# A fused two-layer graph network: another order of the second layer's matmul steps, and other places for its side work

## The chip, the cores and the metric

The kernel runs on one core of a Trainium2 chip. The metric is device time in microseconds; the time before is the median of three runs. A profile is one more execution, recorded instruction by instruction.

The engines are called as the profile calls them: PE is TensorE's matmul, PEld its weight load (the two overlap), DVE is VectorE, ACT ScalarE, POOL GpSimd, and SP the queue that issues nearly all transfers. Each engine works through its own list in order. They meet through semaphores. Matmuls write to PSUM, which has eight banks of 128 x 512 fp32; only DVE and ACT read PSUM back into SBUF.

## The reference

128 graphs of 128 nodes with 512 features, all fp32. Layer 0 is a mean over neighbours, layer 1 a diffusion with attention-like weights; each is followed by a residual and a layer norm.

```python
# layer 0: x = layernorm(x + gnn0(x, adj, W))
deg = jnp.sum(adj, axis=-1, keepdims=True)
agg = jnp.einsum('bij,bjf->bif', adj, x) / jnp.maximum(deg, EPS)
cat = jnp.concatenate([x, agg], axis=2)
out = jax.nn.relu(jnp.einsum('bnf,of->bno', cat, W))

# layer 1: x = layernorm(x + gnn1(x, adj, ...))
Xw = X @ Wv + bv
sj, si = Xw @ aw[:d, 0], Xw @ aw[d:, 0]
e = leaky_relu(sj[:, None, :] + si[:, :, None] + ab[0], 0.2)
alpha = A * jnp.exp(e)
transition = alpha / (jnp.sum(alpha, axis=-1, keepdims=True) + 1e-12)
H, Xk = 0, X
for k in range(3):
    H = H + Xk @ Wk[k] + bk[k]
    Xk = jnp.einsum('bij,bjd->bid', transition, Xk)
out = jax.nn.relu(H)
```

## The kernel before

Four graphs make a group; there are 32 groups (`NG`). Layer 0 goes through all of them, then layer 1. The result of layer 0 goes to memory (`yds`) and comes back.

**Products.** The wide product of layer 1 (x with the three matrices `Wk` and two score columns, laid out as 4 x 385 columns) is computed with seven block products in place of eight, each of which again has seven inner products in place of eight. The outer products are the generators `o1` to `o7`, all made by `outer`. An inner product is one *step*: one matmul of 128 x 128 by 128 x 385, which the profile records as two weight loads and two matmuls. `O5.3` is the third step of outer product 5.

A product works in the four banks of its *lane*, called X, Y, W, Z: lane 1 (the banks `bA`) runs O1, O5, O7 and the combine, lane 0 (`bB`) runs O2, O6, O4 and O3. In `outer` the seven steps do this:

1. X gets the first inner product; ACT copies it to Y (L628). In O5 ACT has first put the bias into X (L626).
2. Z gets one; it goes to SBUF as `s5` (ACT L634, or DVE L632 in O5).
3. X accumulates; DVE writes X + s5 to W (L637).
4. Y accumulates and is evicted (ACT L660, or DVE L669).
5. X accumulates and is read by `direct` (DVE L663 or L676).
6. W accumulates and is evicted.
7. X accumulates and is evicted.

So X is written in steps 1, 3, 5 and 7, and each of the reads between has to end before the next write. Then the banks change roles: the next product on the lane begins in this one's Y.

`combine` (steps c.1 to c.8, 512 columns wide) applies the transition matrix twice to each of four graphs: first result plus `r` or `c` into `v1` (DVE L846, L847), a copy of the base into PSUM (ACT L849), second result on top, and then the residual with ReLU and row sums (DVE L380).

**Order.** Nothing is scheduled automatically: the program walks through a list of steps written by hand and calls the generators, so PE's order is the list's. `PG` serves group 0 of layer 1, `PB` groups 1 to 30, and `PL` the last one. In `PB` the lower-case names (`c.`, and `o3.7`) belong to the group before. Each list of `PB` has 57 steps: 49 products and 8 of the combine; I call it a round.

**Side work.** Everything else has a *place*: twice the number of the step, counted from the round's first step, after which it is issued; an even place comes before the evictions that a step leaves to `late`, an odd one after. A round is 114 places, so place 243 of one round is place 15 of the round after the next. `PLACES_B` holds them. The names:

- `load_left`, `load_y`, `load_adj`: transfers in, on SP (tiles `xb`, `y`, `ag`); `y_store`: the transfer out.
- `x_turn` (DVE L259) turns blocks of x; `x_inner`, `x_s1` to `x_s4` (POOL) make the sums of x that the block products need.
- `sum_r`, `sum_c` (POOL) add the block products `s` onto `r` and `c22`.
- `t_scores` (ACT L725, L726, DVE L734, one store), `t_load` (the load of `T`, L792), `t_exp` (ACT L799, L800), `t_sums` (POOL L805, DVE L807, L810, ACT L808), `t_norm` (ACT L817 and a store to `sd`), `t_back` (loads of `sb`), `t_turn` (DVE L825): they make the transition matrix `TT` for the next round's combine.
- `ln_mean`, `ln_scales` (POOL L499, L510 to L512), `ln_var` (ACT L504), `ln_apply` (ACT L517): the layer norm of rows that the combine has finished.

Of the kernel before, what the change touches and what calls it, by code (L numbers as in the profile page):

```python
# [16 lines left out]
def kernel(  # L17
# [853 lines left out]
    def step(lane, name, g, k):  # L871
        steps.append((lane, name, g, k))
# [4 lines left out]
    PG = ("O5.1 O5.2 O2.5 O5.3 O5.4 O6.1 O2.6 O5.5 O6.2 O5.6 O5.7 O6.3 O7.1 O7.2 O6.4 "  # L877
          "O6.5 O2.7 O7.3 O6.6 O6.7 O7.4 O4.1 O7.5 O4.2 O4.3 O7.6 O4.4 O4.5 O7.7 O4.6 "
          "c.1 c.2 c.3 O4.7 O3.1 c.4 O3.2 c.5 c.6 c.7 O3.3 O3.4 c.8 O3.5 O3.6").split()
    PB = ("O1.1 O1.2 o3.7 O1.3 O2.1 O1.4 O1.5 O2.2 O1.6 O1.7 O2.3 O2.4 O5.1 O2.5 O2.6 O5.2 O5.3 O5.4 O2.7 "  # L880
          "O6.1 O5.5 O6.2 O6.3 O5.6 O5.7 O6.4 O7.1 O7.2 O6.5 O6.6 O7.3 O6.7 O7.4 O4.1 O7.5 O4.2 O4.3 O7.6 "
          "O4.4 O4.5 O7.7 O4.6 c.1 O4.7 O3.1 c.2 O3.2 O3.3 c.3 c.4 c.5 c.6 c.7 c.8 O3.4 O3.5 O3.6").split()
    PL = ("O1.1 o3.7 O1.2 O1.3 O2.1 O2.2 O1.4 O1.5 O1.6 O1.7 O2.3 O2.4 O5.1 O2.5 O2.6 O5.2 O5.3 O5.4 O2.7 O6.1 O5.5 O6.2 "
          "O5.6 O5.7 O6.3 O7.1 O6.4 O6.5 O7.2 O7.3 O6.6 O7.4 O7.5 O6.7 O7.6 O7.7 O3.1 O3.2 O3.3 O3.4 c.1 c.2 c.3 c.4 "
          "c.5 c.6 c.7 c.8 O4.1 O3.5 O4.2 O3.6 O3.7 O4.3 O4.4 O4.5 O4.6 O4.7 x.1 x.2 x.3 x.4 x.5 x.6 x.7 x.8").split()
# [15 lines left out]
    for s in PT:  # L901
        name, k = s.split(".")
        step(int(not s[0].isupper()), {"p74": "P74", "t": "T"}.get(name, name), 0 if s[0] == "O" else NG - 1, int(k))
    base[NG] = len(steps) - PB.index("O5.1")
    LANE = {"O1": 1, "O2": 0, "O5": 1, "O6": 0, "O7": 1, "O4": 0, "C": 1, "O3": 0}
    for g in range(NG):
        base[NG + g] = base[NG] + len(PB) * g
        for s in PL if g == NG - 1 else PB if g else PG:
            name, k = s.split(".")
# [18 lines left out]
    def place_op(n, pos, name, m, *a):  # L928
# [28 lines left out]
        ("a_load", 0): 81, ("load_adj", 1): 43, ("y_store", 0, 0): 161, ("load_y", 0, 0): 105, ("ln_apply", 0, 0): 145,  # L957
    }
    PLACES_B = {
        ("x_s1", 1): 63, ("t_back", 0): 168, ("x_turn", 1, 1, 1): 21, ("ln_apply", 0, 0): 243, ("ln_var", 0, 1): 226,  # L960
        ("x_s2", 1): 79, ("t_scores", 0): 120, ("t_norm", 0): 154, ("sum_r", 0, 0): 85, ("y_store", 0, 0): 275,
        ("t_turn", 0): 189, ("ln_var", 0, 2): 224, ("sum_c", 0, 0): 114, ("x_turn", 1, 0, 0): 11, ("ln_apply", 0, 3): 263,
        ("ln_var", 0, 0): 232, ("t_exp", 0): 143, ("load_left", 2, 1): 68, ("load_y", 0, 0): 175, ("ln_apply", 0, 1): 258,
        ("x_s3", 1): 79, ("sum_r", 0, 1): 87, ("x_inner", 1, 0): 46, ("x_s4", 0): 53, ("x_turn", 1, 0, 1): 27,
        ("t_load", 0): 129, ("ln_apply", 0, 2): 274, ("load_adj", 0): 106, ("load_left", 2, 0): 75, ("load_y", 0, 1): 185,
        ("x_inner", 1, 1): 52, ("ln_scales", 0): 240, ("y_store", 0, 1): 286, ("t_sums", 0): 153, ("x_turn", 1, 1, 0): -4,
        ("ln_mean", 0): 223, ("ln_var", 0, 3): 228, ("sum_c", 0, 1): 110,
    }
    PLACES_M = {
        ("y_store", 0): 250, ("ln_mean",): 214, ("ln_apply", 0): 241, ("ln_apply", 3): 242, ("ln_var", 3): 225,  # L970
# [130 lines left out]
```

## Time and profile before

| | |
|---|---|
| median of three runs | 2068.39 us (2068.28 to 2069.03) |
| the profiled execution, its own time | 2068.23 us |
| its span, first to last instruction | 2066.5 us |
| mean granted TensorE clock | 0.999 |
| layer 1, 830 to 2000 us: PE busy | 1169.93 of 1170.00 us |
| the same stretch: PEld, DVE, ACT, POOL busy | 649.35, 824.49, 612.68, 728.82 us |
| the same stretch: DMA share, moved | 0.47, 109 GB/s |

A row of the timeline gives the start and the length in us, the engine, the line, the operation with its output and inputs, and how many equal instructions in a row were merged (x4). In brackets stands the time that the engine was idle before the row, with what ended it; "issue" is idle time for which the profile shows no releaser. Idle times below 0.15 us are not listed, and the ends of matmuls are modelled, so PE shows as busy across short gaps.

### The profile page before, as it was taken

What the parts mean: (1) busy time and instruction counts of PE and PEld (TensorE: products, weight loads), DVE (VectorE), ACT (ScalarE), POOL (GpSimd) and SP (SyncE); (2) the same over time, 40 slices, a digit from 0 to 9 for tenths busy, and PEclk for the clock granted to TensorE, in tenths of its full rate; (3) what the DMA queues carried; (4) which work ended last, traced back from release to release, by engine and by line L of the source; (5) the groups of instructions that cost most, each with busy time, mean ns of one, the idle gap of its engine ahead of it and who ended that gap; (6) DMA issues with size and microseconds to landing.
All of it is one profiled execution on the core that took longest, in us unless ns stands there. A gap on an engine that the chain in (4) does not pass through costs nothing.

```text
span 2066.5 us, 25981 instructions
## 1 busy us (share of the span) xinstructions
PE 2053.8 (99%) x7108; PEld 1338.4 (65%) x7108; DVE 1515.5 (73%) x3418; ACT 1161.4 (56%) x2872; POOL 1374.6 (67%) x1263
## 2 busy tenths in 40 slices
PE   9999999999999999999999999999999999999998
PEld 6878888888887887555555555555555555555554
DVE  6787777787878777667767767767766766766766
ACT  2666666666666666455455455455455455455454
POOL 5877888887777776756656656656656656656652
PEclk9999999999999999999999999999999999999999
DMA  9777766666667777434534534534534534534623
GB/s 202 176 192 189 187 188 176 158 190 190 165 162 197 181 189 228 108 88 112 129 88 109 132 88 112 128 88 112 128 88 113 128 88 113 128 87 112 129 75 110
DMA packets 431071, 287.14 MB, mean 139 GB/s; under 512 B 155593, under 2 KB 353865, under 8 KB 430924
## 3 DMA queue, kind: packets, MB, share of 16 engines
q1 hardware_dynamic: 429996, 284.15, 55.6%
q10 hardware_dynamic: 800, 1.31, 0.3%
q8 instruction: 56, 0.92, 0.2%
q14 instruction: 91, 0.75, 0.1%
q0 software_dynamic: 128, 0.01, 0.0%
HBM read 191.60 MB, written 93.79 MB: 138 GB/s over the span
## 4 chain that ended last, share of the span: by engine, by line
PE 98%; DMA 1%; DVE 1%; issue 0%; POOL 0%; ACT 0%; ACTq 0%; SPq 0%; DVEq 0%
PE bA L155 51%; PE bB L155 47%; DMA xb<-in_x_dram 0%; DMA big<-in_w0t_dram 0%; PE bA L181 0%; DVE big L1024 0%; DVE c L458 0%; PE bA L167 0%; DVE c L366 0%; ACT y L562 0%; POOL rs L539 0%; DVE dg L730 0%; DVE bA L475 0%; DVE y L380 0%; DVE xl L259 0%
## 5 line engine op out<-in xcount | busy, mean ns | idle before, releaser
L155 PE MATMUL bB<-big,xu 128*128 128x385 f32 (+1 forms) x1806 | 556.8, 433 | 0.1
L155 PEld LDWEIGHTS bB<-big,xu 128*128 128x128 f32 x1806 | 342.6, 190 | 159.8 <-issue 24.4
L155 PE MATMUL bA<-big,xl 128*128 128x256 f32 (+1 forms) x1358 | 406.0, 416 | 0.6 <-DVE bA L475 0.6
L155 PE MATMUL bB<-big,xs 128*128 128x256 f32 (+1 forms) x1316 | 389.0, 416 | 0.0
L155 PEld LDWEIGHTS bA<-big,xl 128*128 128x128 f32 x1358 | 256.5, 189 | 100.5 <-issue 15.3
L155 PEld LDWEIGHTS bB<-big,xs 128*128 128x128 f32 x1316 | 249.6, 190 | 84.1 <-issue 1.7
L155 PE MATMUL bA<-big,xu 128*128 128x256 f32 (+1 forms) x896 | 287.0, 432 | 0.1
L155 PE MATMUL bA<-c,TT 128*128 128x512 f32 x512 | 240.7, 592 | 0.0
L504 ACT ACTIVATE junk<-y,mv 128x512 bf16<-128x512 f32 x252 | 181.7, 721 | 88.9 <-POOL mv L499 82.6
L499 POOL TENSOR_SCALAR mv<-mv 128x4 f32<-128x4 f32 x63 | 14.4, 228 | 313.0 <-DVE y L380 313.0
L155 PEld LDWEIGHTS bA<-big,xu 128*128 128x128 f32 x896 | 166.5, 189 | 76.6 <-DVE bA L397 5.0
L517 ACT ACTIVATE y<-y,mv,rstd 128x512 f32<-128x512 f32 x252 | 204.7, 814 | 3.6 <-POOL mv L512 1.7
L637 DVE TENSOR_TENSOR bB<-bB,s 128x385 f32<-128x385 f32 x128 | 72.6, 567 | 170.9 <-ACT s L634 73.4
L380 DVE SCALAR_TENSOR_TENSOR y<-bA,y 128x512 f32<-128x512 f32 x253 | 165.7, 681 | 12.0 <-PE bA L155 7.4
L155 PE MATMUL bB<-big,xl 128*128 128x385 f32 (+1 forms) x462 | 172.1, 480 | 0.4 <-ACT bA L456 0.4
L805 POOL TENSOR_TENSOR T<-ag,T 128x512 f32<-128x512 f32 x31 | 39.5, 1274 | 198.7 <-ACT T L800 145.8
L155 PE MATMUL bA<-big,xs 128*128 128x385 f32 x448 | 167.9, 491 | 0.0
L155 PEld LDWEIGHTS bA<-c,TT 128*128 128x128 f32 x512 | 96.8, 189 | 88.8 <-issue 47.6
L270 POOL TENSOR_TENSOR xs<-xl 128x896 f32<-128x896 f32 x63 | 131.4, 2085 | 21.4 <-PE bB L155 21.4
L849 ACT COPY bA<-r 128x512 f32<-128x512 f32 x62 | 36.5, 589 | 190.7 <-DVE big L847 190.6
L282 POOL TENSOR_TENSOR xu<-xu,xs 128x896 f32<-128x896 f32 x63 | 131.5, 2087 | 9.3 <-PE bB L155 9.3
L278 POOL TENSOR_TENSOR xl<-xu,xl 128x896 f32<-128x896 f32 x63 | 133.4, 2117 | 1.1
(206 smaller groups left out, 3614.2 us busy)
## 6 DMA issues: line engine op xcount, KB each, us to landing
xb<-in_x_dram SPq DMA_DIRECT2D x256, 128.0 KB, 3.8
y<-in_x_dram SPq DMA_DIRECT2D x64, 512.0 KB, 4.3
yd<-y SPq DMA_DIRECT2D x64, 512.0 KB, 3.0
xb<-yd SPq DMA_DIRECT2D x256, 128.0 KB, 6.5
y<-yd SPq DMA_DIRECT2D x64, 512.0 KB, 6.8
out_dram<-y SPq DMA_DIRECT2D x62, 512.0 KB, 3.3
ag<-in_adj_dram SPq DMA_DIRECT2D x63, 256.0 KB, 6.0
sb<-sd SPq DMA_DIRECT2D x252, 64.0 KB, 3.3
```

Of the source, the lines that this page charges most:

```text
L155: nc.tensor.matmul(dst, lhsT, rhs, start=start, stop=True, skip_group_check=True)
L270: S_.tensor_add(xs[n][:, 0], xl[n][:, 0], xl[n][:, 1])
L278: S_.tensor_sub(xl[n][:, 0], xu[n][:, 0], xl[n][:, 0])
L282: S_.tensor_sub(xu[n][:, 1], xu[n][:, 1], xs[n][:, 1])
L380: V.scalar_tensor_tensor(y, t, 0.0, y, ALU.max, ALU.add, accum_out=mvs[n][:, b, 0:1])
L499: S_.tensor_scalar(mvs[n][:, :, 0], mvs[n][:, :, 0], -1.0 / F, None, ALU.mult)
L504: L_.activation(junk, ys[n, b // 2][:, b % 2], AF.Square, bias=mvs[n][:, b, 0:1], accum_out=mvs[n][:, b, 1:2])
L517: L_.activation(y, y, AF.Identity, bias=mvs[n][:, b, 0:1], scale=rstds[n][:, b : b + 1])
L637: V.tensor_add(W, X, s5)
L805: S_.tensor_mul(T, adjs[NG + g], T)
L849: L_.copy(to[b], row(b, 254, 766, 1))
```

## The change

The list `PB` is replaced by another order of the same 57 steps, and `PLACES_B` by other places for the same pieces of side work. `PG`, `PL`, the other tables of places and all the functions stay as they are. The entries of `PLACES_B` are written in another order, which means nothing.

```diff
-    PB = ("O1.1 O1.2 o3.7 O1.3 O2.1 O1.4 O1.5 O2.2 O1.6 O1.7 O2.3 O2.4 O5.1 O2.5 O2.6 O5.2 O5.3 O5.4 O2.7 "
-          "O6.1 O5.5 O6.2 O6.3 O5.6 O5.7 O6.4 O7.1 O7.2 O6.5 O6.6 O7.3 O6.7 O7.4 O4.1 O7.5 O4.2 O4.3 O7.6 "
-          "O4.4 O4.5 O7.7 O4.6 c.1 O4.7 O3.1 c.2 O3.2 O3.3 c.3 c.4 c.5 c.6 c.7 c.8 O3.4 O3.5 O3.6").split()
+    PB = ("O1.1 o3.7 O1.2 O1.3 O1.4 O2.1 O2.2 O1.5 O1.6 O1.7 O2.3 O2.4 O5.1 O2.5 O5.2 O5.3 O2.6 O2.7 O6.1 "
+          "O5.4 O5.5 O6.2 O5.6 O6.3 O5.7 O6.4 O7.1 O6.5 O6.6 O7.2 O7.3 O6.7 O4.1 O7.4 O7.5 O4.2 O4.3 O7.6 "
+          "O4.4 O4.5 O7.7 O4.6 c.1 O4.7 O3.1 c.2 O3.2 c.3 O3.3 c.4 c.5 c.6 c.7 c.8 O3.4 O3.5 O3.6").split()
```

```diff
     PLACES_B = {
-        ("x_s1", 1): 63, ("t_back", 0): 168, ("x_turn", 1, 1, 1): 21, ("ln_apply", 0, 0): 243, ("ln_var", 0, 1): 226,
-        ("x_s2", 1): 79, ("t_scores", 0): 120, ("t_norm", 0): 154, ("sum_r", 0, 0): 85, ("y_store", 0, 0): 275,
-        ("t_turn", 0): 189, ("ln_var", 0, 2): 224, ("sum_c", 0, 0): 114, ("x_turn", 1, 0, 0): 11, ("ln_apply", 0, 3): 263,
-        ("ln_var", 0, 0): 232, ("t_exp", 0): 143, ("load_left", 2, 1): 68, ("load_y", 0, 0): 175, ("ln_apply", 0, 1): 258,
-        ("x_s3", 1): 79, ("sum_r", 0, 1): 87, ("x_inner", 1, 0): 46, ("x_s4", 0): 53, ("x_turn", 1, 0, 1): 27,
-        ("t_load", 0): 129, ("ln_apply", 0, 2): 274, ("load_adj", 0): 106, ("load_left", 2, 0): 75, ("load_y", 0, 1): 185,
-        ("x_inner", 1, 1): 52, ("ln_scales", 0): 240, ("y_store", 0, 1): 286, ("t_sums", 0): 153, ("x_turn", 1, 1, 0): -4,
-        ("ln_mean", 0): 223, ("ln_var", 0, 3): 228, ("sum_c", 0, 1): 110,
+        ("ln_apply", 0, 1): 257, ("ln_var", 0, 3): 227, ("t_scores", 0): 121, ("x_turn", 1, 0, 1): 26, ("x_s1", 1): 65,
+        ("t_back", 0): 164, ("x_turn", 1, 1, 1): 25, ("x_inner", 1, 1): 63, ("sum_r", 0, 1): 86, ("t_turn", 0): 189,
+        ("ln_var", 0, 1): 225, ("x_s2", 1): 80, ("t_norm", 0): 155, ("y_store", 0, 1): 287, ("sum_r", 0, 0): 84,
+        ("sum_c", 0, 0): 116, ("x_turn", 1, 0, 0): 10, ("ln_apply", 0, 3): 257, ("ln_var", 0, 0): 233, ("t_exp", 0): 138,
+        ("load_left", 2, 1): 86, ("y_store", 0, 0): 261, ("t_load", 0): 128, ("load_y", 0, 0): 179, ("x_s3", 1): 74,
+        ("x_inner", 1, 0): 52, ("ln_apply", 0, 2): 284, ("ln_var", 0, 2): 228, ("load_adj", 0): 116, ("x_s4", 0): 50,
+        ("load_left", 2, 0): 57, ("load_y", 0, 1): 187, ("ln_mean", 0): 221, ("ln_scales", 0): 241, ("t_sums", 0): 151,
+        ("ln_apply", 0, 0): 244, ("x_turn", 1, 1, 0): 6, ("sum_c", 0, 1): 97,
     }
```

## The prediction

> **What bounds the kernel now.** I read the page first, then the list of waits, then the chain in order of time, and then two short stretches of the timeline: an ordinary round of the second layer and its last round.
>
> ```profile
> span 2066.5 us, 25981 instructions
> ...
> PE 2053.8 (99%) x7108; PEld 1338.4 (65%) x7108; DVE 1515.5 (73%) x3418; ACT 1161.4 (56%) x2872; POOL 1374.6 (67%) x1263
> ...
> PE 98%; DMA 1%; DVE 1%; issue 0%; POOL 0%; ACT 0%; ACTq 0%; SPq 0%; DVEq 0%
> ```
>
> TensorE is the bound, and by the page it is never idle. The chain in order of time gives the length of a round: the twelve matmul records at the end of a combine (c.3 to c.8) begin once a round.
>
> ```profile
> 1339.41 5.15 PE bA L155 x12
> ...
> 1378.13 5.15 PE bA L155 x12
> ```
>
> That is 38.72 us a round. What would it be with no loss at all? Four records take 1.29 us (any "x4" row of the chain), so one step of 385 columns, two records, takes 0.647 us; six steps of 512 columns take 5.15, so one takes 0.858. A round has 49 of the first and 8 of the second: 31.70 + 6.86 = 38.57. So a round loses about 0.16 us that no busy share shows, and this is all there is to win. An ordinary round shows where:
>
> ```profile
> 1504.52 1.46 PE L155 MATMUL bA<-big,xu 128*128 128x385 f32 x4
> ...
> 1506.01 0.56 DVE L663 TENSOR_TENSOR r<-bA,s 128x385 f32<-128x385 f32 x1 [0.27 <-PE bA L155]
> ...
> 1507.03 0.81 ACT L517 ACTIVATE y<-y,mv,rstd 128x512 f32<-128x512 f32 x1
> ...
> 1507.75 0.85 ACT L660 COPY r<-bA 128x385 f32<-128x385 f32 x2
> 1507.75 1.46 PE L155 MATMUL bB<-big,xu 128*128 128x385 f32 x4
> ...
> 1508.48 0.50 ACT L626 COPY bA<-beta 128x385 f32<-128x385 f32 x1
> ...
> 1509.10 0.30 PEld L155 LDWEIGHTS bA<-big,xs 128*128 128x128 f32 x2 [0.51 <-issue]
> ```
>
> L626 puts the bias into the bank of O5.1. ScalarE reaches it late, behind the normalisation L517 and two evictions L660, and ends at 1508.98. O5.1 was due at 1507.75 + 4 x 0.3235 = 1509.04; its weights load at 1509.10, and the matmul after it comes at 1509.85 where 1507.75 + 6 x 0.3235 = 1509.69 was due: 0.16 lost. (It is the same in every round: among the weight loads from 890 to 1960 us, the group bA<-big,xs idles 13.7 us before its loads without a named releaser, 27 times this 0.51.) So this copy has to end 0.22 us before the slot to cost nothing. The same stretch shows O1.5 (from 1505.17) read by L663 until 1506.57, and O1.7, which writes the same bank again, not due before 1507.11: no loss.
>
> The last round runs another list (PL), in which only O1.6 stands between O1.5 and O1.7:
>
> ```profile
> 2008.76 3.02 PE L155 MATMUL bA<-big,xu 128*128 128x385 f32 x8
> ...
> 2010.25 0.56 DVE L663 TENSOR_TENSOR r<-bA,s 128x385 f32<-128x385 f32 x1 [1.44 <-PE bA L155]
> ...
> 2010.86 0.30 PEld L155 LDWEIGHTS bA<-big,xu 128*128 128x128 f32 x2 [0.62 <-DVE r L663]
> ...
> 2011.62 1.46 PE L155 MATMUL bB<-big,xu 128*128 128x385 f32 x4
> 2011.82 0.48 ACT L660 COPY r<-bA 128x385 f32<-128x385 f32 x1 [0.44 <-PE bA L155]
> 2012.19 0.49 ACT L626 COPY bA<-beta 128x385 f32<-128x385 f32 x1
> ```
>
> The four steps O1.4 to O1.7 begin at 2008.76 and O2.3 was due at 2008.76 + 4 x 0.647 = 2011.35; it begins at 2011.62. The wait for L663 cost 0.27 us.
>
> **The change, part by part.** No instruction is added or removed. PB serves 30 rounds (groups 1 to 30), so 0.14 us a round is 4.1 us, which is 0.2%.
>
> *O1.5 to O1.7.* Old list: O1.5 O2.2 O1.6 O1.7. New list: O1.5 O1.6 O1.7, the neighbourhood of the last round. O1.5's result is read by L663, and O1.7 accumulates into the same bank. From O1.5's start: L663 begins at 0.85 (2010.25 less 2009.40) and ends at 1.41; the next weights load 0.05 later, at 1.46; O1.7 was due at 2 x 0.647 = 1.29. That is 0.17 late, and a start from standstill costs about 0.10 more (the rest of the 0.27). In the old list O1.7 is due at 1.94, half a microsecond after the read. Does VectorE come to L663 in time in the new round? Ahead of it now stand L637 of O1.3 (four steps earlier: from 0.85 to 1.42 of O1.3), transposes of 0.70 and 0.71 and the small L734 of 0.21, done by about 2.9, while O1.5's result is there at 4 x 0.647 + 0.85 = 3.44. Yes. So 30 x 0.27 = 8.1 us. Bounds: nothing, if the read were covered, and 0.37, if a second start from standstill of 0.10 went with it. I take 0.27, measured on the same pair of instructions.
>
> The Trainium skill (Perfetto Trace Analysis, Optimizing Tensor Performance, Matmuls) asks to rotate independent matmul groups through PSUM banks so that an eviction overlaps the next group's matmuls. The new list does rotate, with O1.6 on another bank between; by that rule alone this term would be 0 and the time about 2068.9. The row of the last round shows that one matmul of 0.647 between is too little cover.
>
> *Every other pair of this kind.* In each product the steps 1-3, 3-5 and 5-7 use one bank with a read between. By the row above three places apart is free and two is not. Counted in both lists, all pairs of all seven products are three or more apart, old and new, but for O1's 5-7 in the new one. Price 0; one more start from standstill, 0.10 x 30 = 3, is the upper bound.
>
> *The bias copy L626.* ln_apply of row 0 moves from place 243 to 244, which puts L517 behind the eviction of O1.6, no longer ahead of it. From O1.6's start: L660 from 0.85 to 1.33; L517 from 1.23 (a ScalarE instruction starts some 0.10 before the row ahead ends, as at 1508.48) to 2.04; O1.7's L660, ready at 0.647 + 1.12 = 1.77 (2011.82 against a due start of 2010.70), from 1.94 to 2.42; L626 from 2.31 to 2.81. It needs 0.22 more: 3.03. O5.1 is due three steps behind the late O1.7, at 0.647 + 0.27 + 3 x 0.647 = 2.86. So it still waits 0.17. It was 0.16 in 29 rounds (group 1's ran clear, as nothing is normalised there) and will be 0.17 in 30, the last round included, since the moved L517 of group 29 falls there: 5.1 - 4.6 = +0.5 us. Bounds: -4.6, if it goes altogether, and +8.3, if it grew to 0.43 (0.17 plus the 0.27 that O1.7's delay lends it).
>
> *The side work.* VectorE's and POOL's moves stay within a few steps, and neither sets a step: x_inner and x_s1 to x_s4 make operands of the next round; sum_c runs at 97 and 116 and is wanted at 121 and in the next combine. t_exp moves from 143 to 138: L734 starts at 1504.85 and the load of T (L792) is issued at 1507.02 and lands 3.4 later, so 5.6 us from L734 to T. From place 7 to place 24 there are now 8.5 steps, 5.5 us, plus 0.44 of new waits: ScalarE waits a tenth or two at most. Behind it stand four L799, L800, two L517, and then a copy whose user is five steps on: covered. On SP's queue a second-half load of xb goes out later (place 86, used 17 steps or about 12 us on; landing 6.6), the first half goes ahead of the output store and both y loads, and load_adj leaves at 116, some 12 us before its use, landing 6.7. The copies sd and sb (2.4 and 3.4) are followed by other loads than before but still have two microseconds before L825. Price 0.
>
> *Sum.* 8.1 + 0.5 = 8.6. The profiled execution took 2068.23 us, 1.7 more than its span; 2068.23 + 8.6 = 2076.8. The median of the runs is 0.16 above it: 2077.0. A round should take 38.72 - 0.16 + 0.27 + 0.17 = 39.00 us.
>
> **The rivals.** *The read is covered and the bias copy is free* (ends faster): O1.7 would need L663 to end 0.15 before its slot, 1.14 after O1.5's start instead of 1.41, and L626 0.17 earlier. Then only the old loss goes: 2068.4 - 4.6 = 2063.8. For it speaks that the new list spreads other pairs wider (O3's 1-3 from three places to four); against it, L663 took 0.56 in every round. Chance 5%.
>
> *Only the bias copy gets free*: 2068.4 + 8.1 - 4.6 = 2071.9. It needs L517 to slip 0.2 us to another place in ScalarE's queue; the order of instructions puts it between the two L660. 7%.
>
> *T comes late*: ScalarE blocks at L799 with the copies of O6 and O2 behind it. Its cover is about 1.5 us; if T landed 2 us later than its 3.4, half a microsecond a round would be lost on top: 2077.0 + 15 = 2092. DMA is 47% busy in this stage, and SP's queue is empty when L736 is issued, which speaks against it. 4%.
>
> **How the numbers follow.** The forecast has 84%, its own range 2075.5 to 2079. The runs shown lie within 0.04% of each other, so about 0.2% (4.1 us) can be told from no change. Slower takes the forecast, the late T and nearly all of the second rival's neighbourhood above 2072.5; that rival itself, at 2071.9, lies 0.17% up and counts mostly as same. Faster takes the first rival, in part: faster 0.04, same 0.06, slower 0.90. The range goes from 2071.8, the second rival, to 2080, the forecast plus its upper bound of one more restart in each round.
>
> **What would show it.** In the changed profile the runs of twelve records should begin 39.0 us apart, not 38.72. L663 should be named as what held a weight load some 31 times in place of 2, by about 0.6 us of PEld idle time each. L626 should stand 0.2 us or less before its matmul's slot, with an L517 between two L660 ahead of it. If PEld shows no wait for L663 in the rounds, the first step is wrong; if the rounds are 38.8, the second is; if L799 starts right behind a wait for its load and the steps behind it slip, the third is.

## The result, and the profile after

The changed kernel takes 2076.64 us (median of five runs, 2076.59 to 2076.90), the kernel before in the same comparison 2068.28. The ratio is 1.0041, with a 95% interval of 1.0030 to 1.0052: slower by 8.4 us. Forecast were 2077.0.

First the page of the changed kernel: its span, the busy times, and the group of weight loads for lane 1 from `xu`.

```profile
span 2074.9 us, 25863 instructions
...
PE 2060.9 (99%) x7108; PEld 1338.2 (64%) x7108; DVE 1522.0 (73%) x3418; ACT 1163.6 (56%) x2872; POOL 1374.7 (66%) x1263
...
L155 PEld LDWEIGHTS bA<-big,xu 128*128 128x128 f32 x896 | 164.4, 190 | 87.8 <-DVE r L663 19.2
```

PE is again at 99%, though 8 us were lost: a kernel that is bound by PE can lose time that its busy share doesn't show. The last number of the group tells it. Before, this group's idle time had L397 as its main releaser; now it is L663, the read of O1.5's bank. The page of before has for the same group

```profile
L155 PEld LDWEIGHTS bA<-big,xu 128*128 128x128 f32 x896 | 166.5, 189 | 76.6 <-DVE bA L397 5.0
```

The lists of PEld's waits (in total, times, longest) have L663 first in the kernel before, then in the changed one, as

```profile
PEld bA L155 <- DVE r L663: 0.6, 1, 0.6
```

```profile
PEld bA L155 <- DVE r L663: 19.2, 31, 0.6
```

31 times in place of once: the 30 rounds of PB and the last round. A round in the timeline:

```profile
1237.13 2.38 PE L155 MATMUL bA<-big,xu 128*128 128x385 f32 x6
...
1237.98 0.56 DVE L663 TENSOR_TENSOR r<-bA,s 128x385 f32<-128x385 f32 x1 [0.67 <-PE bA L155]
1238.59 0.30 PEld L155 LDWEIGHTS bA<-big,xu 128*128 128x128 f32 x2 [0.62 <-DVE r L663]
1238.62 0.48 ACT L660 COPY r<-bA 128x385 f32<-128x385 f32 x1 [0.81 <-PE bA L155]
...
1239.00 0.82 ACT L517 ACTIVATE y<-y,mv,rstd 128x512 f32<-128x512 f32 x1
...
1239.34 1.46 PE L155 MATMUL bB<-big,xu 128*128 128x385 f32 x4
1239.71 0.47 ACT L660 COPY r<-bA 128x385 f32<-128x385 f32 x1
1240.08 0.49 ACT L626 COPY bA<-beta 128x385 f32<-128x385 f32 x1
...
1240.68 0.30 PEld L155 LDWEIGHTS bA<-big,xs 128*128 128x128 f32 x2 [0.50 <-issue]
```

O1.5, O1.6 and O1.7 are the six records from 1237.13; O2.3 was due at 1237.13 + 6 x 0.3235 = 1239.07 and begins at 1239.34: 0.27 lost, as in the last round of before. Then the bias copy L626 ends at 1240.57, O5.1's weights load at 1240.68, and the next matmul on the other lane (1241.43 in the trace) was due at 1239.34 + 6 x 0.3235 = 1241.28: 0.15 lost, where it was 0.16.

The chain in order of time gives the round (ten of the combine's last records, since O3.3 now stands among them):

```profile
1265.52 4.29 PE bA L155 x10
...
1304.52 4.29 PE bA L155 x10
```

39.00 us, as forecast; 38.72 before.

### The profile page after: what moved, and what is told of

Same layout as the page of the kernel before. It is cut to its first block, busy times and chain, and to the rows that moved or that the text cites. A ratio compares the mean times of both kernels' runs of the same rounds, so it can differ in the third digit from the quotient of the medians.

```text
span 2074.9 us, 25863 instructions
## 1 busy us (share of the span) xinstructions
PE 2060.9 (99%) x7108; PEld 1338.2 (64%) x7108; DVE 1522.0 (73%) x3418; ACT 1163.6 (56%) x2872; POOL 1374.7 (66%) x1263
## 4 chain that ended last, share of the span: by engine, by line
PE 98%; DMA 1%; DVE 1%; issue 0%; POOL 0%; ACT 0%; ACTq 0%; SPq 0%; DVEq 0%
PE bA L155 51%; PE bB L155 47%; DMA xb<-in_x_dram 0%; DMA big<-in_w0t_dram 0%; PE bA L181 0%; DVE big L1024 0%; DVE c L458 0%; PE bA L167 0%; DVE c L366 0%; ACT y L562 0%; POOL rs L539 0%; DVE bA L475 0%; DVE y L380 0%; DVE xl L259 0%; DVE st L546 0%
## 5 line engine op out<-in xcount | busy, mean ns | idle before, releaser
L155 PE MATMUL bA<-big,xl 128*128 128x256 f32 (+1 forms) x1358 | 401.4, 416 | 0.3 <-DVE bA L475 0.3
L155 PE MATMUL bB<-big,xs 128*128 128x256 f32 (+1 forms) x1316 | 394.1, 416 | 0.0
L155 PE MATMUL bA<-c,TT 128*128 128x512 f32 x512 | 245.7, 592 | 0.0
L517 ACT ACTIVATE y<-y,mv,rstd 128x512 f32<-128x512 f32 x252 | 201.5, 813 | 3.6 <-POOL mv L512 1.7
L155 PE MATMUL bA<-big,xs 128*128 128x385 f32 x448 | 173.1, 491 | 0.0
L637 DVE TENSOR_TENSOR bB<-bB,s 128x385 f32<-128x385 f32 x128 | 72.6, 567 | 129.0 <-ACT r L660 51.3
L849 ACT COPY bA<-r 128x512 f32<-128x512 f32 x62 | 36.6, 590 | 190.7 <-DVE big L847 190.6
```

The costliest lines, as they stand in the source:

```text
L155: nc.tensor.matmul(dst, lhsT, rhs, start=start, stop=True, skip_group_check=True)
L517: L_.activation(y, y, AF.Identity, bias=mvs[n][:, b, 0:1], scale=rstds[n][:, b : b + 1])
L637: V.tensor_add(W, X, s5)
L849: L_.copy(to[b], row(b, 254, 766, 1))
```

## Experiments

Ten kernels, each timed in several rounds beside the kernel before. In the diffs, "before" and "changed" say from which kernel the edit starts.

| run | edit | median us | ratio to before, 95% interval |
|---|---|---|---|
| e1 | changed, O1.5 a step earlier | 2076.69 | 1.0040 (1.0028 to 1.0053) |
| e2 | changed, L517 back to 243 | 2072.42 | 1.0019 (1.0010 to 1.0028) |
| e3 | changed, O1.5 a step earlier, L517 at 254 | 2064.21 | 0.9979 (0.9970 to 0.9988) |
| e4 | before, L517 at 254 | 2063.85 | 0.9977 (0.9968 to 0.9986) |
| e5 | new list, old places | 2071.74 | 1.0016 (1.0008 to 1.0025) |
| e6 | old list, new places | 2082.34 | 1.0070 (1.0057 to 1.0082) |
| e7 | before, longer inner evictions | 2072.95 | 1.0023 (1.0013 to 1.0032) |
| e8 | changed, longer inner evictions | 2077.64 | 1.0046 (1.0033 to 1.0058) |
| e9 | e4, with O1.5 O1.6 O1.7 in a row | 2072.08 | 1.0018 (1.0009 to 1.0027) |
| e10 | e4, with O4.1 and O4.3 two apart | 2068.76 | 1.0003 (0.9994 to 1.0012) |

The kernel before measured 2068.41 beside e1 to e4, 2068.33 beside e5 to e8 and 2068.45 beside e9 and e10.

### e1: give O1.5 its distance back

```diff
-    PB = ("... O1.4 O2.1 O2.2 O1.5 O1.6 O1.7 ...
+    PB = ("... O1.4 O2.1 O1.5 O2.2 O1.6 O1.7 ...
```

> The changed kernel with O1.5 one step earlier in PB (O2.1 O1.5 O2.2 O1.6 O1.7), so that two matmuls stand between O1.5 and O1.7 again; places untouched. Both theories expect the wait for L663 to go from 30 rounds (0.27 each). Theory (the two waits share their cover): L626 stands behind an L517 that sits between the two L660, and O1.7's delay has been lending it 0.27 us; without it the bias copy is 0.15 + 0.27 = 0.42 late in each round, so the time stays at 2076.6, within 0.6. Rival (the waits are separate terms): the bias copy keeps its 0.15 and the time falls by 30 x 0.27 = 8.0 to 2068.6. Second rival (the loss sits in the moved transfers and POOL work): 2076.6 too, but with the wait for L663 gone and the bias copy still at 0.15, and another wait in the rounds.

Measured 2076.69: no gain at all, though PEld no longer waits for L663 in any round. The timeline of e1 says where the 8 us went:

```profile
1199.62 0.48 ACT L660 COPY r<-bA 128x385 f32<-128x385 f32 x1 [0.16 <-PE bA L155]
1200.00 0.81 ACT L517 ACTIVATE y<-y,mv,rstd 128x512 f32<-128x512 f32 x1
...
1200.72 0.47 ACT L660 COPY r<-bA 128x385 f32<-128x385 f32 x1
...
1201.08 0.49 ACT L626 COPY bA<-beta 128x385 f32<-128x385 f32 x1
1201.68 0.30 PEld L155 LDWEIGHTS bA<-big,xs 128*128 128x128 f32 x2 [0.77 <-issue]
```

L517 still sits between the two L660, so L626 comes when it came; only its slot, the time at which PE is due there, is 0.27 earlier. O5.1's weights now load 0.77 after the load before, in place of 0.50: 0.42 lost in place of 0.15. The two waits are not two terms of a sum. The first one hides as much of the second as it lasts. This excludes the rival of separate waits (2068.6); the second rival is excluded by e3.

### e2: move L517 ahead of the evictions

```diff
-        ("ln_apply", 0, 0): 244,      # changed
+        ("ln_apply", 0, 0): 243,
```

> The changed kernel with ln_apply of row 0 back from place 244 to 243 alone, so that L517 stands ahead of O1.6's L660. Theory: the bias copy then ends in time, as in the last round of before, and its 0.15 goes from 30 rounds, -4.5, while the wait for L663 stays: 2072.1. Rival (ScalarE's load as such makes the copy late, not the place of L517): 2076.6, no change.

Measured 2072.42. One place, which is half a step, is worth 4.2 us:

```profile
1197.46 0.82 ACT L517 ACTIVATE y<-y,mv,rstd 128x512 f32<-128x512 f32 x1
...
1198.38 0.48 ACT L660 COPY r<-bA 128x385 f32<-128x385 f32 x1
...
1199.30 0.48 ACT L660 COPY r<-bA 128x385 f32<-128x385 f32 x1 [0.44 <-PE bA L155]
1199.67 0.49 ACT L626 COPY bA<-beta 128x385 f32<-128x385 f32 x1
...
1200.28 0.31 PEld L155 LDWEIGHTS bA<-big,xs 128*128 128x128 f32 x2 [0.34 <-issue]
```

L517 runs while ScalarE would have waited for O1.6, the second L660 waits for PE and not for ScalarE, and the bias is there in time. An idle time of PEld is still listed, 0.34, but the matmul after it is not late (1199.10 + 1.94 = 1201.04, its start in the trace).

### e3 and e4: no wait left

```diff
     # e3, from the changed kernel: the edit of e1, and
-        ("ln_apply", 0, 0): 244,
+        ("ln_apply", 0, 0): 254,
     # e4, from the kernel before: this alone
-        ("ln_apply", 0, 0): 243,
+        ("ln_apply", 0, 0): 254,
```

> The changed kernel with both: O1.5 one step earlier and ln_apply of row 0 at place 254, behind the bias copy L626. Theory: neither wait is left, rounds of 38.57 us, 30 x (0.27 + 0.15) = 12.6 less: 2064.0, under the kernel before. Rival (separate waits, or another cause in the side work): at best 2068.6, rounds of 38.72 or more.

> The kernel before with one number changed: ln_apply of row 0 from place 243 to 254, behind the bias copy. Theory: the only loss of its rounds, 0.16 at O5.1 in 29 of them, goes: 2068.3 - 4.6 = 2063.7. Rival (the copy is late whatever stands around it, or something else takes the place of the wait): 2068.3.

Measured 2064.21 and 2063.85: both faster than the kernel before and the changed one. The chain of e4 in order of time:

```profile
1222.33 5.15 PE bA L155 x12
...
1260.90 5.15 PE bA L155 x12
```

38.57 us, the round without loss that was worked out from the rows of before. So both lists reach the round without loss once L517 is out of the bias copy's way and O1.5 has its distance; the other moves of the new list neither cost nor win anything in these rounds.

### e5 and e6: the list alone, the places alone

e5 has the new `PB` with the old `PLACES_B`, e6 the old `PB` with the new `PLACES_B`.

> The new list PB with the old places. Theory: the pair O1.5-O1.7 costs its 0.27 in 30 rounds (+8.0), while L517 at the old place 243 now falls ahead of O1.6's L660, so the bias copy is in time and its 0.16 goes from 29 rounds (-4.6): 2068.4 + 3.4 = 2071.8. Rival (the bias copy keeps its wait, list and places each have a price of their own): 2076.4. Rival (the loss is in the places): 2068.4.

> The old list PB with the new places. Theory: no wait for L663, since two matmuls stand between O1.5 and O1.7; but L517 at place 244 sits between the two L660 and nothing lends the bias copy time, so it is late by 0.42 to 0.45 in place of 0.16, +8.3 in all, and a copy L628 after t_exp's earlier place may be late by up to 0.16 in each round, up to +4.6: 2076.7 to 2081.5. Rival (the places alone are harmless, ScalarE is busy only half the time): 2068.4 to 2070.

e5 measured 2071.74, as expected: the list alone costs 3.4, made of +8.0 and -4.6. e6 measured 2082.34, 0.8 over the upper end of what was expected. Its bias copy loses 0.42 in each round, as in e1, and there is a second wait, of 0.19 where 0.16 was allowed for:

```profile
1204.90 1.28 ACT L799 ACTIVATE T<-T,si 128x128 f32<-128x128 f32 x4
...
1209.53 0.20 ACT L808 ACTIVATE rw<-rw 128x4 f32<-128x4 f32 x1 [0.91 <-DVE rw L807]
1209.64 0.47 ACT L628 COPY bB<-bB 128x385 f32<-128x385 f32 x1
...
1210.16 0.30 PEld L155 LDWEIGHTS bB<-big,xs 128*128 128x128 f32 x2 [0.54 <-ACT bB L628]
```

ScalarE stands at L808, waiting for DVE's row sums (t_sums, at 151 in place of 153), and O6.1's copy L628 is queued behind it. Before, the copy went first:

```profile
1514.58 0.46 ACT L628 COPY bB<-bB 128x385 f32<-128x385 f32 x1
1515.12 0.21 ACT L808 ACTIVATE rw<-rw 128x4 f32<-128x4 f32 x1
```

So the piece that the expectation named, t_exp, is not the one: its L799 starts with no idle time. List and places do not add up: alone they cost 3.4 and 14.0, together 8.4. In the changed kernel the wait for L628 does not arise, and the bias copy waits 0.15 and not 0.42.

### e7 and e8: is there more room?

The change is described as an order with room for longer evictions. In both kernels the evictions inside a product (L628, L634, L637; all products but O5) were made to move 480 columns; nothing uses the added ones.

```diff
-        s5 = halves()[:, :BW]
+        EW = BW if bias else 480; sw = halves()[:, :EW]; s5 = sw[:, :BW]
+        wX, wY, wW, wZ = [t[:, :EW] for t in lane]
...
-        L_.copy(Y, X)
+        L_.copy(wY, wX)
...
-            L_.copy(s5, Z)
+            L_.copy(sw, wZ)
...
-        V.tensor_add(W, X, s5)
+        V.tensor_add(wW, wX, sw)
```

> The kernel before with three evictions inside each product but O5 (L628, L634, L637) moving 480 columns in place of 385; the added columns are used by nothing. Going by 512 columns in 0.589 us (L849) and 385 in 0.464 (L628), each takes some 0.09 longer. Theory: several of them stand in a row on ScalarE ahead of L626, so the bias copy slips by their sum, 0.16 to about 0.5 a round: 2068.4 + 12 = 2080, more than the changed kernel with the same evictions. Rival (evictions have cover everywhere but at the pair O1.5-O1.7): 2068.4 to 2071.

> The changed kernel with the same longer evictions (480 columns in L628, L634, L637 of all products but O5). Theory: its order has the room that its description names, and its two waits do not depend on these evictions: L663 is not among them, and the ones ahead of L517 end in time. 2076.6 to 2077.2, so faster than the kernel before under equal evictions, by about 3. Rival (no more room than before): 2080 or more, still slower than the kernel before with the same.

The evictions grew as meant (L634 from 0.474 to 0.551 us, L637 from 0.567 to 0.667). The kernel before pays 4.6 for it, the changed one 1.0. The rounds of the changed kernel stay at 38.99 us, those of the kernel before grow from 38.72 to 38.86; the 1.0 is lost ahead of 845 us, where layer 1 begins, and took e8 0.4 over the upper end of what was expected. So the changed kernel has more room in its rounds. It need not come from the list: in the kernel before, part of the price goes through L517 (below), and e7's edit was not tried with L517 at 254. But 12 was expected for the kernel before, and it did not fall behind the changed one. The timeline of e7 shows the error:

```profile
1236.71 0.56 ACT L634 COPY s<-bB 128x480 f32<-128x480 f32 x1 [0.61 <-PE bB L155]
1237.16 0.82 ACT L517 ACTIVATE y<-y,mv,rstd 128x512 f32<-128x512 f32 x1
...
1239.23 0.30 PEld L155 LDWEIGHTS bA<-big,xs 128*128 128x128 f32 x2 [0.59 <-issue]
```

L634 waits for PE first. The longer evictions ahead of it end in that idle time, and only L634's own 0.08 reaches the bias copy: 0.59 in place of 0.51. That is 2.3 us in 29 rounds, half of the 4.6. Another 0.05 a round, 1.6 us in all, is lost in the combine, which the expectation did not have: L634 and L637 of O3 are longer there, so the base copy L849 starts 0.18 later, and the weights of a second result wait for it. First e7, then the kernel before:

```profile
1227.57 0.30 PEld L155 LDWEIGHTS bA<-big,TT 128*128 128x128 f32 x2 [0.61 <-ACT bA L849]
```

```profile
1264.99 0.42 PEld L155 LDWEIGHTS bA<-big,TT 128*128 128x128 f32 x2 [0.43 <-ACT bA L849]
```

Whether still longer evictions turn the order of the two kernels was not tried.

### e9 and e10: the price of a short distance by itself

Both start from e4, whose rounds have no wait.

```diff
     # e9
-    O2.1 O1.4 O1.5 O2.2 O1.6 O1.7
+    O2.1 O1.4 O2.2 O1.5 O1.6 O1.7
     # e10
-    O7.4 O4.1 O7.5 O4.2 O4.3
+    O7.4 O7.5 O4.1 O4.2 O4.3
```

> The kernel before with ln_apply of row 0 at place 254 (rounds without any wait, 2063.9), and with O2.2 put ahead of O1.5, so that O1.5 O1.6 O1.7 follow each other. It measures the pair by itself. Theory: 30 x 0.267 = 8.0 more, 2071.9. Rival (some of the 0.27 in the changed kernel came from its other moves): less than 2070.

> The kernel before with ln_apply of row 0 at place 254 (2063.9), and with O7.5 ahead of O4.1, so that O4.1 and O4.3 stand two places apart, with the copy L628 on ScalarE (0.46 us) between them. It tests the rule for another pair and engine. Theory: the copy ends 0.85 + 0.46 = 1.31 after O4.1's start, weights load 0.05 later, 0.07 behind the slot at 1.29, and the start from standstill adds 0.10: 30 x 0.17 = 5.2, 2069.1. Rival (only the pair with L663 is short; a ScalarE copy is covered): 2063.9.

Taken against the kernel before of the same comparison, e9 is 8.2 above e4 (+3.6 against -4.6) and e10 4.9 (+0.3 against -4.6); expected were 8.0 and 5.2. So the pair O1.5-O1.7 costs the same 0.27 here as in the changed kernel and in the last round of before, and a pair with a ScalarE copy between costs 0.17:

```profile
1214.43 0.46 ACT L628 COPY bB<-bB 128x385 f32<-128x385 f32 x1 [4.05 <-PE bB L155]
1214.94 0.30 PEld L155 LDWEIGHTS bB<-big,xl 128*128 128x128 f32 x2 [0.52 <-ACT bB L628]
```

## Why the prediction was right

**O1.5 to O1.7: +8.1.** Right. The wait came in all 30 rounds with the 0.27 read off the last round of before, and e9 shows it alone. The lower bound, nothing, needed the read to be covered; a single matmul on another bank was too little cover, as the row had it.

**The other pairs: 0.** Right for the changed kernel, and e10 shows that the count of places was the right thing to count: a pair made two places apart costs, on another engine too.

**The bias copy: +0.5.** The mechanism was right, the size too large. The wait was 0.15, not 0.17, in 30 rounds, against 0.156 in 29, 4.6 us in place of 4.5: no change. That O1.7's delay lends the copy 0.27 was worked out in the prediction, as the way to its upper bound; e1 shows that it does.

**The side work: 0.** Right in the rounds: L799 starts right behind the copy L628 (1242.01 in the trace, with no idle time), so T was in time; in two of the rounds it waits 0.3 for its load, and no matmul is late for it. Besides L663 one more releaser of PEld is new, L847 (30 times, 0.24 each), but 0.24 is also what the weight loads of 512 columns show with "issue", and no matmul is late there. Not right at the end of the kernel. The last two matmuls start 7.76 later than before (2064.56 against 2056.80), but the span is 8.4 longer: from these matmuls to the end it takes 10.3 us in place of 9.7. (In these two executions layer 1 also began 0.2 earlier after the change than before, so the rounds themselves cost 8.0.) The last waits of SP, for the final stores, end later. All kernels here with the new places have a longer end (10.2 to 10.3) than those with the old (9.6 to 9.7); since e5 has 9.7 and e6 10.3, it goes with the places and not with the list. Why these stores land later was not tried, and stays open. So it is luck that the total came out this close: the bias term was half a microsecond too high, and the end, which had no term, took about as much.

**The rivals.** "Only the bias copy gets free" was worked out at 2071.9. The chip gives this time when exactly that is done: 2072.42 in e2 and 2071.74 in e5. "The read is covered and the bias copy is free" was 2063.8; e3 has 2064.21. So the rivals' mechanisms and prices were right, and neither is what the change does. T was late by 0.3 in two rounds, and at no cost.

**Where the expected gain went.** The changed kernel's rounds do take longer evictions at no price (e8 against e7), whether by its list or by its places. With evictions as they are, the old rounds had only 0.16 us to win. The new ones shortened one distance below what its read needs, and put L517 where the bias copy can't be early.

## What to carry to other kernels

When one engine is bound and shows 99%, work out from the rows what a round would take with no loss, and compare it with the round's length: the difference is all that reordering can win in a round, and here it was 0.16 of 38.72 us. Count, for each bank, how many slots lie between a write, the read of it and the next write; a list of matmuls and three row lengths give the answer before anything runs. Waits that follow each other on one engine need not add up: undo one alone and the next may take its place (e1), so look at what stands ahead of the late instruction in its own queue, where moving a single instruction by half a step was worth 4 us (e2).

## What was not expected of the hardware

The idle time that the profile lists before a weight load is not the loss, but the loss follows from it. With 0.34 us listed the matmuls are on time (e2); 0.50 costs 0.15 (the changed kernel), 0.52 costs 0.17 (e10), 0.62 costs 0.27 (the changed kernel) and 0.77 costs 0.42 (e1). So for steps of 385 columns in these rounds each listed idle time beyond 0.35 is lost one for one, whoever ended it. For steps of 512 columns the number is another: 0.43 cost nothing there (the kernel before), and 0.61 cost 0.05 (e7). In particular a first record that is late by only 0.17 costs 0.27: in the changed kernel the two records of O1.7 begin at 1238.59 and 1239.02 in the trace, 0.43 apart where 0.32 is usual, so the second comes another 0.10 late after this start from standstill.
